# Scatters of rows into expert lists, issued one at a time between the matmuls' accompanying steps

## The chip, the core and the metric

One NeuronCore of a Trainium2 chip runs the kernel. Its engines work side by side, each through its own queue of instructions in order: PE (TensorE, matmuls), DVE (VectorE), ACT (ScalarE), POOL (GpSimd) and SP (SyncE, here only a queue that starts DMA transfers). They wait for one another by semaphores. The metric is the device time of one execution in microseconds (us); less is better.

## The reference

The input is x, 8 batches of 256 tokens with 128 numbers each (2048 tokens in all). Two layers follow one another, each a conditioning step and a feed-forward network (FFN) with 8 experts of 512 hidden units, and each adds its result to x:

```python
x = x + _L0_ffn_ref(_L0_cond_ref(x, ...), ...)   # all 8 experts for every token, weighted by gates above a threshold
x = x + _L1_ffn_ref(_L1_cond_ref(x, ...), ...)   # the 2 best experts of each token

def _L1_ffn_ref(x, gate_w, w1, b1, w2, b2, gamma, beta):
    xn = (x - mu) * jax.lax.rsqrt(var + LN_EPS) * gamma + beta
    probs = jax.nn.softmax(jnp.einsum('bld,de->ble', xn, gate_w), axis=-1)
    w, idx = jax.lax.top_k(probs, TOP_K)                 # TOP_K = 2
    w = w / jnp.sum(w, axis=-1, keepdims=True)
    ...
    h = jax.nn.gelu(jnp.einsum('bld,edh->eblh', xn, w1) + b1[:, None, None, :], approximate=False)
    out_e = jnp.einsum('eblh,ehd->ebld', h, w2) + b2[:, None, None, :]
    return jnp.einsum('ble,ebld->bld', cw, out_e) + residual
```

The first FFN is dense: every expert sees every token. In the second a token needs two experts of eight. The kernel computes only those, and for that it sorts the tokens by expert.

## The kernel before

**Tiling.** The 2048 tokens are 16 tiles of 128. The list UNITS cuts them into five units: units 0, 1 and 2 have four tiles each (512 tokens), units 3 and 4 have two each (256 tokens).

**First FFN (function layer).** For each unit u and each expert e there are four matmuls into the hidden layer (hp, L784), each followed by a GELU on ACT (L786), and four that lead back to 128 numbers (yp, L764, in second). The second half runs one expert behind the first. Accumulate multiplies each yp by the gates of its tokens on DVE (L752) and adds it to acc (L754). The gates come from DRAM as a row copied to all partitions, gbc (L744, a transfer on SP, four buffers). When the last expert of a unit is in, a generator, adapt, is put into the queue behind.

**Steps beside the matmuls.** The function pump is called after each matmul (in the units of two tiles after every second one). It advances the generator at the head of behind by one step. So what adapt does for unit u stands in the program between the matmuls of the unit after it. Adapt(u) transposes acc on PE (fp, L455), applies the adapter of the batch's language (adp, L581, and dp, L588), and normalises twice. Each normalising has a power on POOL: rstd_l and rstd_f, L471. It writes the normalised rows twice into zr, once for each of the two experts (L474, and a copy by ACT), takes a sum on POOL (resid, L609) and writes each row's place in the output into a spare column (copies on POOL, L612). Then it transposes the rows (znp, L617), computes the second layer's logits (L628), picks the two best experts, and counts, with a matmul by a triangle (kp, L659 and L660), the place that each token gets in its expert's list.

**Scatters.** These places, pos, are made on DVE (L674). For each of the two experts and each tile one transfer from POOL, an indirect DMA (L676), writes 128 rows of 520 bytes to xs in DRAM, each to its place. A unit of four tiles has eight scatters, a unit of two has four, 32 in all. They stand in the program one behind the other, four (or two) in one step of adapt and the rest in the next.

**Second FFN.** After unit 2 the lists of 17 full tiles are known, after unit 3 four more, after unit 4 the rest (SLOTS). Each such tile k has one expert. Its rows are loaded from xs (xt, L814) and its expert's weights from DRAM (wt, L822), both on SP, by fetch. The first load of a new stretch of lists (k = 0, 17, 21) waits for all scatters of the units up to it. Fetch(k) also reads the tile's place and expert from the list into registers. Eight tiles are fetched (function early) just ahead of the first FFN's last yp in the program. Then come, for each tile, a transpose (xtp, L829), the hidden layer (hps, L840, with a GELU on ACT, L842), the way back (yps, L849), a sum on DVE (yt, L852), a scaling on ACT (L853), and a scatter of the result to the output's buffer ys from POOL (L854, 36 of them). At the end ys is read back, added up and stored.

**Order.** The program's text gives the order in which work is recorded. A planner then places the instructions on the engines' queues by when it reckons them to be ready, so an instruction that it thinks late can land behind one that was recorded after it, on SP and POOL among others. On the chip each queue is worked off in that fixed order: what waits at its head holds everything behind it.

Of the kernel before, what the change touches and what calls it, by code (L numbers as in the profile page):

```python
# [15 lines left out]
SYNC = mybir.DependencyInfo(mybir.DependencyClass.Sync, mybir.DependencyReason.DATA)  # L16
# [6 lines left out]
P = 128  # L23
# [7 lines left out]
SLOTS = {2: 17, 3: 21, 4: 39}  # L31
E, HC = 8, 4
# [12 lines left out]
SEARCH = 16  # L45
SEARCH_GAP = 3
CHAIN_GAP = 5
GATES_GAP = 16
DRAIN = 4
LEAD = 5  # L50
# [18 lines left out]
def tile_adaln_ffn_d2(ctx: ExitStack, tc: tile.TileContext, x, ptype, lang, cols, b1v,  # L69
                      w10, w20, w11d, w21d, lw1, lw2, lgb, out):  # L70
    nc = tc.nc
# [34 lines left out]
    for e in range(E):  # L106
        t = first.tile([P, HC * P], F32, tag="w1", name=f"w10_{e}")
        nc.sync.dma_start(out=t, in_=w10[e])
        w10s.append(t)
        t = const.tile([P, HC, D], F32, name=f"w20_{e}")  # L110
# [42 lines left out]
    for b in range(B):  # L153
        at = nc.values_load(lgi[0:1, b:b + 1], engines=(SP,), min_val=0, max_val=NL - 1,
                            skip_runtime_bounds_check_because="a language's number")
        for lst, name, src, rows, width in (
# [3 lines left out]
            t = const.tile([rows, width], F32, name=f"{name}_{b}")  # L160
# [19 lines left out]
    fwd, bwd, rows = fwd[:B, :], bwd[:B, :], top[:B, :]  # L180
# [40 lines left out]
    for g in range(NG):  # L221
# [8 lines left out]
        if not g:  # L230
            nc.tensor.matmul(bvp.rearrange("p c a -> p (c a)"), lhsT=ones[:A, :],
                             rhs=diag.rearrange("k c a -> k (c a)"), start=True, stop=True)
# [266 lines left out]
    xs = dram.tile([ROWS + GT * P, RW], F32, name="xs")  # L499
    ys = dram.tile([2 * NT * P, D], F32, name="ys")  # L500
    last, lists, scatters, tiles = [None], {}, [], []
    used = const.tile([P, E], F32, name="used")
    nc.gpsimd.memset(used, 0.0)

# [61 lines left out]
    def adapt(u, acc):  # L566
# [99 lines left out]
        if u in SLOTS:  # L666
            counts = small.tile([P, E], F32, tag="counts", name=f"counts{u}", bufs=2)
            nc.vector.tensor_copy(counts, kp[:, nt, :])
        for s, oh in enumerate((oh1, oh2)):
            wh = small.tile([P, GT, E], F32, tag="s", name=f"wh{u}_{s}")[:, :nt, :]  # L670
            nc.vector.tensor_tensor(wh, oh, at, ALU.mult)
            pos = small.tile([P, GT], I32, tag="pos", name=f"pos{u}_{s}")[:, :nt]
            with nc.allow_low_precision("whole numbers below 2 ** 24"):
                nc.vector.tensor_reduce(pos, wh, AX.X, ALU.add)  # L674
            for t in range(nt):
                move = nc.gpsimd.indirect_dma_start(  # L676
                    out=xs, out_offset=bass.IndirectOffsetOnAxis(ap=pos[:, t:t + 1], axis=0),
                    in_=zr[s][:, t, :], in_offset=None)
                tc.declare_no_dep(move.ins, group="scattered", reason="no two tokens share a row")
                tc.add_to_no_dep_group("scattered", move.ins)  # L680
                scatters.append((u, move.ins.name))
                tc.add_to_no_dep_group(f"scattered {u}", move.ins)
                for v in range(u):
                    if v in SLOTS:
                        tc.declare_no_dep(move.ins, group=f"loads {v}", reason="full tiles get no more rows")
            yield
        if u in SLOTS:

# [10 lines left out]
            if u < NU - 1:  # L699
# [5 lines left out]
                nc.vector.tensor_tensor(new, new, f, ALU.min)  # L705
                nc.vector.tensor_tensor(used, used, new, ALU.add)


    behind = deque()
    waiting = deque()  # L710

    def run(key, steps):
# [6 lines left out]
    def pump():  # L719
        if gd0:  # L720
            n = next(ready)
            if not n:
                gates0.append(gd0[0])
            if waiting and n >= 0 and n % DRAIN == 0:
                waiting.popleft()()
        if behind:
            if next(behind[0], done) is done:
                behind.popleft()

    def finished(key):  # L730
        while key not in done:
            pump()

    def layer(name, act, sources, w1s, w2s, cb1, cb2, gates, before, then, early):

        accs, missing = {}, [E] * NU

        def accumulate(u, e, y, bias):  # L740
            g, o, nt = UNITS[u]
            n, t0 = nt * P, e * NT + g * GT + o
            gbc = work.tile([P, GN], F32, tag="gbc", name=f"gbc_{name}{u}_{e}", bufs=4)[:, :n]
            nc.sync.dma_start(out=gbc, in_=gates[0][t0:t0 + nt, :].rearrange("t p -> (t p)").partition_broadcast(P))  # L744
            begun = u in accs
            if not begun:
                accs[u] = work.tile([P, GN], F32, tag="acc", name=f"acc_{name}{u}", bufs=3)[:, :n]
            part = work.tile([P, GN], F32, tag="part", name=f"part_{name}{u}_{e}")[:, :n] if begun else accs[u]
            if bias is None:
                nc.vector.tensor_tensor(part, y, gbc, ALU.mult)  # L750
            else:
                nc.vector.scalar_tensor_tensor(part, y, bias, gbc, ALU.add, ALU.mult)  # L752
            if begun:
                nc.vector.tensor_tensor(accs[u], accs[u], part, ALU.add)  # L754
            missing[u] -= 1
            if not missing[u]:
                behind.append(run((name, u), then(u, accs[u])))

        def second(u, e, hT):
            nt = UNITS[u][2]  # L760
            n = nt * P
            yp = psy.tile([P, GN], F32, tag="y", name=f"yp_{name}{u}_{e}")[:, :n]
            for c in range(HC):
                nc.tensor.matmul(yp, lhsT=w2s[e][:, c, :], rhs=hT[:, c, :], start=(c == 0), stop=(c == HC - 1))  # L764
                if nt == GT or c % 2:
                    pump()
            b2 = col[:, cb2 + e:cb2 + e + 1]
            if gates:
                accumulate(u, e, yp, b2)
            else:  # L770
                y = scratch(f"y_{name}{u}_{e}").rearrange("p a b -> p (a b)")[:, :n]
                nc.scalar.activation(y, yp, AF.Identity, bias=b2)  # L772
                waiting.append(lambda u=u, e=e, y=y: accumulate(u, e, y, None))


        due = deque()
        for u, (g, o, nt) in enumerate(UNITS):
            n = nt * P
            finished((before, g))
            for e in range(E):  # L780
                hT = work.tile([P, HC, GN], F32, tag="hT", name=f"hT_{name}{u}_{e}")[:, :, :n]
                for c in range(HC):
                    hp = psb.tile([P, GN], F32, tag="big", name=f"hp_{name}{u}_{e}_{c}")[:, :n]
                    nc.tensor.matmul(hp, lhsT=w1s[e][:, c * P:(c + 1) * P], rhs=sources[g][:, o * P:o * P + n],  # L784
                                     start=True, stop=True)
                    nc.scalar.activation(hT[:, c, :], hp, act,  # L786
                                         bias=col[:, cb1 + e * HC + c:cb1 + e * HC + c + 1])
                    if nt == GT or c % 2:
                        pump()
                if due:  # L790
                    second(*due.popleft())
                due.append((u, e, hT))
        early()
        second(*due.popleft())


    def listing(k):

        return min(u for u in SLOTS if k < SLOTS[u])
# [7 lines left out]
    def fetch(k):  # L807
        u = listing(k)
        rows, i = lists[u], k - SLOTS.get(u - 1, 0)
        at = nc.values_load(rows[0:1, 0, i:i + 1], engines=(SP,), min_val=0, max_val=ROWS,  # L810
                            skip_runtime_bounds_check_because="at most ROWS, a difference of counts")
        ek = expert(k, SP)
        xt = work.tile([P, RW], F32, tag="xt", name=f"xt{k}", bufs=LEAD + 2 * AHEAD + 2)
        move = nc.sync.dma_start(out=xt, in_=xs[bass.ds(at, P), :])  # L814
        for v, name in scatters if k in (0, *SLOTS.values()) else ():
            if v <= u:
                tc.add_manual_dep(move.ins, name, SYNC, reason="rows of full tiles")
        for v in range(u + 1, NU):
            tc.declare_no_dep(move.ins, group=f"scattered {v}", reason="full tiles get no more rows")
        tc.add_to_no_dep_group(f"loads {u}", move.ins)  # L820
        wt = first.tile([P, HC * P], F32, tag="w1", name=f"wt{k}")
        nc.sync.dma_start(out=wt, in_=w11d.rearrange("e p w -> (e p) w")[bass.ds(ek * P, P), :])  # L822
        return k, xt, wt
# [12 lines left out]
    def hidden(k, xt, wt, xc, b1):  # L836
        hp = psb.tile([P, HC, P], F32, tag="big", name=f"hps{k}")
        hT = work.tile([P, HC, P], F32, tag="scr", name=f"hs{k}", bufs=NSCR)
        for c in range(HC):
            nc.tensor.matmul(hp[:, c, :], lhsT=wt[:, c * P:(c + 1) * P], rhs=xc, start=True, stop=True)  # L840
        for c in range(HC):
            nc.scalar.activation(hT[:, c, :], hp[:, c, :], AF.Gelu, bias=b1[:, c:c + 1])  # L842
        return k, xt, hT
# [25 lines left out]
    def ahead(k):  # L869

        if k < SURE:
            finished(("first", listing(k)))
            fetched.append(fetch(k))

    def early():
# [91 lines left out]
```

## Time and profile before

| | us |
|---|---|
| runs shown | 388.47, 380.01, 388.97 (median 388.47) |
| the execution that was profiled | 380.68 |
| its span in the profile | 379.0 |
| POOL: 32 scatters into xs (L676) | 31.5 busy, 986 ns each |
| POOL: 36 scatters into ys (L854) | 35.2 busy, 977 ns each |
| PE: hp (L784) and yp (L764) of the first FFN | 121.2 and 120.6 busy |
| PE: hps (L840) and yps (L849) of the second FFN | 39.2 and 39.6 busy |
| PE's last matmul ends | 355.4 |

All times in the profile are from the span's start. A line of the timeline gives start, length, engine, line of the program, operation, what is written and what is read, how often in a row (x4), and in brackets how long the engine was idle before it and what ended that wait. A fp32 matmul shows as two records, or passes. Line numbers are those of the kernel before.

### The profile page before, as it was taken

Reading aid. Unit: us, or ns where it says so; the run is one execution under the profiler, and the core shown is the slowest. Engines: PE = TensorE matmul, PEld = TensorE weight load, DVE = VectorE, ACT = ScalarE, POOL = GpSimd, SP = SyncE. Lnnn points to the kernel's source line nnn. Section 1 sums busy time; section 2 is a strip of 40 time slices with the busy share of each in tenths; the row PEclk is TensorE's granted clock in tenths of the full one; section 3 lists DMA queues with packets and bytes.
Section 4 is the critical chain, followed back from the end, with each engine's and each line's share of the span. In section 5 each row is a group of like instructions: output and inputs, shape, how many; then the busy total and the mean of one; then the engine's idle time right before and its main releaser. Section 6 shows DMA issues by size and latency. Waiting matters only on the chain. (4 is left out here: it accounts for less than half of the span.)

```text
span 379.0 us, 5911 instructions
## 1 busy us (share of the span) xinstructions
PE 345.8 (91%) x1596; PEld 233.0 (61%) x1596; DVE 195.0 (51%) x801; ACT 167.0 (44%) x387; POOL 94.5 (25%) x142
## 2 busy tenths in 40 slices
PE   6799999999999999999999999989989879999900
PEld 6695444444444445445445688857869769999900
DVE  4775565542245675565512474847576644333305
ACT  2166434553542244223443244425635637567800
POOL 8100000000000030650350021262045565444530
PEclk9999999999999999999999999999999998999975
DMA  6935999005222101210130001126543554566136
GB/s 189 382 84 150 368 379 356 4 0 148 69 77 102 56 30 55 63 49 30 56 69 14 28 29 42 36 65 175 151 121 107 162 162 121 168 187 173 47 117 244
DMA packets 33603, 46.12 MB, mean 122 GB/s; under 512 B 5349, under 2 KB 16375, under 8 KB 33569
## 3 DMA queue, kind: packets, MB, share of 16 engines
q1 hardware_dynamic: 29024, 39.26, 34.6%
q0 software_dynamic: 2304, 4.37, 3.2%
q10 hardware_dynamic: 2240, 2.10, 1.6%
q8 instruction: 14, 0.23, 0.3%
q14 instruction: 21, 0.16, 0.1%
HBM read 31.57 MB, written 14.39 MB: 121 GB/s over the span
## 5 line engine op out<-in xcount | busy, mean ns | idle before, releaser
L786 ACT ACTIVATE hT_first<-hp_first,col 128x512 f32<-128x512 f32 (+1 forms) x160 | 93.4, 601 | 103.3 <-PE hp_first L784 102.3
L784 PE MATMUL hp_first<-poolT,w 128*128 128x512 f32 (+1 forms) x320 | 121.2, 513 | 1.3 <-DVE xr L591 0.7
L764 PE MATMUL yp_first<-hT_first,w 128*128 128x512 f32 (+1 forms) x320 | 120.6, 511 | 0.0
L784 PEld LDWEIGHTS hp_first<-poolT,w 128*128 128x128 f32 x320 | 58.8, 190 | 44.2 <-issue 38.2
L764 PEld LDWEIGHTS yp_first<-hT_first,w 128*128 128x128 f32 x320 | 59.0, 190 | 42.5 <-issue 38.6
L676 POOL DMA_INDIRECT xs<-zr,pos x32 | 31.5, 986 | 64.3 <-DVE pos L674 27.9
L842 ACT ACTIVATE hs<-hps,b 128x128 f32<-128x128 f32 x144 | 40.6, 365 | 11.2 <-PE hps L840 5.3
L854 POOL DMA_INDIRECT ys<-yt,xt x36 | 35.2, 977 | 40.9 <-ACT hs L842 28.3
L849 PE MATMUL yps<-w,hs 128*128 x288 | 39.6, 283 | 2.5 <-DVE row L558 2.4
L840 PE MATMUL hps<-xc,wt 128*128 128x128 f32 x288 | 39.2, 280 | 1.1 <-issue 1.1
L849 PEld LDWEIGHTS yps<-w,hs 128*128 128x128 f32 x288 | 35.7, 195 | 4.3 <-issue 3.5
L752 DVE SCALAR_TENSOR_TENSOR part_first<-yp_first,col,gbc_first 128x512 f32<-128x512 f32 (+1 forms) x28 | 17.2, 614 | 40.4 <-PE yp_first L764 39.9
L840 PEld LDWEIGHTS hps<-xc,wt 128*128 128x128 f32 x288 | 36.0, 196 | 0.8 <-issue 0.6
L853 ACT ACTIVATE yt<-yt,xt 128x128 f32<-128x128 f32 x36 | 14.6, 405 | 23.3 <-issue 15.0
L754 DVE TENSOR_TENSOR acc_first<-acc_first,part_first 128x512 f32<-128x512 f32 (+1 forms) x35 | 20.1, 580 | 0.5
L579 POOL MEMSET ha<- 1x512 f32 x5 | 2.6, 516 | 67.6 <-PE dp L588 67.4
L406 POOL DMA_DIRECT2D gd_L<-gT_L x1 | 0.6, 649 | 74.3 <-DVE gT_L L404 74.3
L833 DVE COPY b<-col 128x4 f32 x36 | 7.2, 200 | 23.0 <-ACT hs L842 17.7
L852 DVE TENSOR_TENSOR yt<-yps,b2all 128x128 f32<-128x128 f32 x36 | 10.5, 291 | 14.8 <-PE yps L849 7.1
L831 DVE TENSOR_SCALAR xc<-xtp,col 128x128 f32<-128x128 f32 x36 | 14.4, 401 | 4.0 <-PE xtp L829 2.4
L772 ACT ACTIVATE y_first<-yp_first,col 128x512 f32<-128x512 f32 x8 | 5.5, 687 | 24.2 <-PE yp_first L764 24.2
L420 DVE TENSOR_SCALAR_CACHE_REDUCE fl<-logit,tr 128x128 f32<-128x128 f32 x46 | 13.5, 343 | 0.6
(205 smaller groups left out, 304.2 us busy)
## 6 DMA issues: line engine op xcount, KB each, us to landing
wt<-in_w_dram SPq DMA_DIRECT2D x36, 256.0 KB
xs<-empty SPq DMA_DIRECT2D x1, 8580.0 KB
w<-in_w_dram SPq DMA_DIRECT2D x24, 256.0 KB
gbc_first<-gd_L SPq DMA_DIRECT2D x24, 256.0 KB
xt<-xs SPq DMA_DIRECT2D x36, 65.0 KB
gbc_first<-gd_L SPq DMA_DIRECT2D x16, 128.0 KB
lgb<-in_lgb_dram SPq DMA_DIRECT2D x8, 128.0 KB
yg<-ys ACTq DMA_DIRECT2D x4, 256.0 KB
```

Of the source, the lines that this page charges most:

```text
L676: move = nc.gpsimd.indirect_dma_start(out=xs, out_offset=bass.IndirectOffsetOnAxis(ap=pos[:, t:t + 1], axis=0), in_=zr[s][:, t, :], in_off ...
L752: nc.vector.scalar_tensor_tensor(part, y, bias, gbc, ALU.add, ALU.mult)
L754: nc.vector.tensor_tensor(accs[u], accs[u], part, ALU.add)
L764: nc.tensor.matmul(yp, lhsT=w2s[e][:, c, :], rhs=hT[:, c, :], start=(c == 0), stop=(c == HC - 1))
L784: nc.tensor.matmul(hp, lhsT=w1s[e][:, c * P:(c + 1) * P], rhs=sources[g][:, o * P:o * P + n], start=True, stop=True)
L786: nc.scalar.activation(hT[:, c, :], hp, act, bias=col[:, cb1 + e * HC + c:cb1 + e * HC + c + 1])
L831: nc.vector.tensor_scalar(xc, tp, col[:, C_LG:C_LG + 1], col[:, C_LB:C_LB + 1], ALU.mult, ALU.add)
L840: nc.tensor.matmul(hp[:, c, :], lhsT=wt[:, c * P:(c + 1) * P], rhs=xc, start=True, stop=True)
L842: nc.scalar.activation(hT[:, c, :], hp[:, c, :], AF.Gelu, bias=b1[:, c:c + 1])
L849: nc.tensor.matmul(yp, lhsT=hT[:, c, :], rhs=w21[:, bass.ds(ek, 1), c * D:(c + 1) * D], start=(c == 0), stop=(c == HC - 1))
L853: nc.scalar.activation(yt, yt, AF.Copy, scale=xt[:, D + 1:D + 2])
L854: move = nc.gpsimd.indirect_dma_start(out=ys, out_offset=bass.IndirectOffsetOnAxis(ap=xt.bitcast(I32)[:, D:D + 1], axis=0), in_=yt, in_off ...
```

## The change

The scatters leave the step that computes the places. Adapt puts them into a queue, moves. Every second call of pump (MOVE_GAP) takes one from it and records it, ahead of the step of the generator. The function moved(u) records all that are left of the units up to u: it is called for unit u - 1 before unit u computes its places, and for a tile's unit before that tile is fetched. Each scatter gets one wait more: recent holds the name of the matmul of an expert (hp, yp or the last of a tile's hps) that was recorded last, and the scatter waits until PE has done it. The transfers themselves, their number and their data stay as they are.

```diff
+MOVE_GAP = 2
...
+    moves = deque()
+    recent = [None]
...
+        moved(u - 1)
         for s, oh in enumerate((oh1, oh2)):
...
             for t in range(nt):
-                move = nc.gpsimd.indirect_dma_start(
-                    out=xs, out_offset=bass.IndirectOffsetOnAxis(ap=pos[:, t:t + 1], axis=0),
-                    in_=zr[s][:, t, :], in_offset=None)
-                tc.declare_no_dep(move.ins, group="scattered", reason="no two tokens share a row")
...
+                moves.append((u, pos[:, t:t + 1], zr[s][:, t, :]))
             yield
...
+    def scatter(u, pos, zr):
+        move = nc.gpsimd.indirect_dma_start(
+            out=xs, out_offset=bass.IndirectOffsetOnAxis(ap=pos, axis=0), in_=zr, in_offset=None)
+
+        tc.add_manual_dep(move.ins, recent[0], SYNC, reason="one after another")
+        tc.declare_no_dep(move.ins, group="scattered", reason="no two tokens share a row")
...
+    def moved(u):
+
+        while moves and moves[0][0] <= u:
+            scatter(*moves.popleft())
...
+    beat = itertools.count()
...
     def pump():
...
+        if not next(beat) % MOVE_GAP and moves:
+            scatter(*moves.popleft())
         if behind:
...
-                nc.tensor.matmul(yp, lhsT=w2s[e][:, c, :], rhs=hT[:, c, :], start=(c == 0), stop=(c == HC - 1))
+                mm = nc.tensor.matmul(yp, lhsT=w2s[e][:, c, :], rhs=hT[:, c, :], start=(c == 0), stop=(c == HC - 1))
+                recent[0] = mm.ins.name
...
-                    nc.tensor.matmul(hp, lhsT=w1s[e][:, c * P:(c + 1) * P], rhs=sources[g][:, o * P:o * P + n],
-                                     start=True, stop=True)
+                    mm = nc.tensor.matmul(hp, lhsT=w1s[e][:, c * P:(c + 1) * P], rhs=sources[g][:, o * P:o * P + n],
+                                          start=True, stop=True)
+                    recent[0] = mm.ins.name
...
-            nc.tensor.matmul(hp[:, c, :], lhsT=wt[:, c * P:(c + 1) * P], rhs=xc, start=True, stop=True)
+            mm = nc.tensor.matmul(hp[:, c, :], lhsT=wt[:, c * P:(c + 1) * P], rhs=xc, start=True, stop=True)
+        recent[0] = mm.ins.name
...
         if k < SURE:
             finished(("first", listing(k)))
+            moved(listing(k))
             fetched.append(fetch(k))
```

In the program that this makes, the orders of PE, DVE and ACT are the same as before. On POOL unit 0's scatters stand among unit 1's rstd_l, resid and rstd_f, the last three of unit 2 among unit 3's, and two of unit 4's behind a scatter into ys each. On SP the order of unit 4's gate rows and of the first tiles' loads differs: before, four gate rows stand among the loads of tiles 0 to 5; now three of these stand ahead of the first load, and the fourth (expert 7) behind the weights of tile 7.

More of the change, by code (lines that the diff above doesn't have):

```diff
@@ L675, in adapt @@
             for t in range(nt):
-                move = nc.gpsimd.indirect_dma_start(
-                    out=xs, out_offset=bass.IndirectOffsetOnAxis(ap=pos[:, t:t + 1], axis=0),
-                    in_=zr[s][:, t, :], in_offset=None)
-                tc.declare_no_dep(move.ins, group="scattered", reason="no two tokens share a row")
[L680 to L685, printed above, removed]
+                moves.append((u, pos[:, t:t + 1], zr[s][:, t, :]))
             yield
@@ L706, in adapt @@
                 nc.vector.tensor_tensor(used, used, new, ALU.add)
+    def scatter(u, pos, zr):
[3 more added lines that the diff above has]
+        tc.declare_no_dep(move.ins, group="scattered", reason="no two tokens share a row")
+        tc.add_to_no_dep_group("scattered", move.ins)
+        scatters.append((u, move.ins.name))
+        tc.add_to_no_dep_group(f"scattered {u}", move.ins)
+        for v in range(u):
+            if v in SLOTS:
+                tc.declare_no_dep(move.ins, group=f"loads {v}", reason="full tiles get no more rows")
+    def moved(u):
+        while moves and moves[0][0] <= u:
+            scatter(*moves.popleft())
     behind = deque()
+    beat = itertools.count()
     waiting = deque()
```

## Prediction

> **What bounds the kernel now.** I read the page's busy table first, then the waits of PE, then the timeline of PE, POOL and SP round each wait that is left.
>
> ```profile
> PE 345.8 (91%) x1596; PEld 233.0 (61%) x1596; DVE 195.0 (51%) x801; ACT 167.0 (44%) x387; POOL 94.5 (25%) x142
> PEclk9999999999999999999999999999999998999975
> ```
>
> TensorE is the bound. It works from some 20 us to 356 us, at full clock but for one dent; the last 23 us are the output's way out. So POOL's 31.5 us of scatters (L676, 32 of 986 ns) cost nothing as such. What counts is whether PE waits. From 20 us to 240 us it doesn't (each 20 us stretch of the table by stretches shows 20.00 us busy, or 19.98 and 19.99). Its later waits, between 240 and 340 us, longest first:
>
> ```profile
> PE yps L849 <- DVE row L558: 2.4, 1, 2.4
> PE znp L617 <- DVE zr L474: 1.5, 3, 0.8
> PE xtp L829 <- DVE xc L831: 1.5, 1, 1.5
> PE hps L840 <- issue: 1.1, 1, 1.1
> PE kp L659 <- DVE sofar L653: 0.9, 1, 0.9
> ```
>
> Columns: total us, times, longest. These and a few below 0.8 us are some 9 us. A faster POOL can gain no more; a later transfer can lose as much as it likes. The place to look at is the hand-over from the first FFN to the second. POOL there, then SP:
>
> ```profile
> 252.73 0.96 POOL L676 DMA_INDIRECT xs<-zr,pos  x1 [0.31 <-issue]
> 257.08 0.73 POOL L471 TENSOR_TENSOR rstd_l<-ve_l,nhalf 128x2 f32<-128x2 f32 x1 [3.39 <-DVE ve_l L469]
> 259.92 0.72 POOL L609 TENSOR_TENSOR resid<-x,xr 128x256 f32<-128x256 f32 x1 [2.11 <-DVE xr L598]
> 260.86 0.71 POOL L471 TENSOR_TENSOR rstd_f<-ve_f,nhalf 128x2 f32<-128x2 f32 x1 [0.22 <-DVE ve_f L469]
> ```
>
> ```profile
> 255.28 0.35 SPq L814 DMA_DIRECT2D xt<-xs  x1
> 255.73 0.37 SPq L744 DMA_DIRECT2D gbc_first<-gd_L  x1
> 266.14 0.38 SPq L744 DMA_DIRECT2D gbc_first<-gd_L  x1
> ```
>
> The first is the eighth and last scatter of unit 2. The first tile's load of rows (xt0) waits for it and goes 2.55 us after its start. The last line is the gate row of unit 4, expert 7 (gbc4_7), which DVE and then PE use here:
>
> ```profile
> 277.84 0.47 DVE L752 SCALAR_TENSOR_TENSOR part_first<-yp_first,col,gbc_first 128x256 f32<-128x256 f32 x1
> 278.84 0.44 PE L455 MATMUL fp<-ident,acc_first 128*128 128x128 f32 x2
> ```
>
> Product, sum into acc, then PE's transpose, with nothing between: PE has no slack here, gbc4_7 has 8 us (landing records put it at 269.7 us).
>
> [...] A scatter is 128 x 520 = 66,560 bytes[...] (landing 2.1 to 2.3 us after the start in most of the 31 scatters that have records). [...] rstd_l of unit 1 starts at 164.36 us, behind eight scatters and a memset without a gap. [...] after the waits at 309.6 to 313.4 us the granted clock is 0.86 and 0.80 in the next two 5 us stretches, and eight passes of yps take 1.81 us in place of 1.06.
>
> **The change part by part.** Built, the changed program has the same order on PE, DVE and ACT; the orders of POOL and SP change.
>
> *Units 0 and 1.* Each keeps 8 scatters at 0.96 us plus 0.30 us of issue. Their waits are for matmuls one pair of pumps apart: two 128x512 matmuls, 1.7 us of PE (eight passes, four matmuls, take 3.4 us from start to start). Unit 0's 8 then take some 18 us, to 172, in place of 10. Behind the fifth, which waits for a matmul that PE ends at 163.1 us, stands rstd_l of unit 1; it starts at 164.3 us, as now (164.36), since it gets ahead of the other three. PE has no wait there. Bounds: nothing either way; taken 0. If that cover were gone, a scatter is 1.26 us.
>
> *Unit 2.* The waits are for matmuls that PE ends at about 243.9, 245.6, 247.7, 250.2, 253.6, 256.2, 258.0 and 259.7 us (positions in the new order, read off PE's timeline). But the last three now stand on POOL behind unit 3's rstd_l, resid and rstd_f, and these wait for DVE. So: rstd_l ends 257.8, sixth scatter 258.1 to 259.1; resid ends 260.6, seventh 260.9 to 261.9; rstd_f 261.95 in place of 260.86 (+1.1 us, straight into PE's wait for zr at 262.1); a copy; eighth at 263.2. Landed 2.2 us later and issued 0.4 us after that, as now: **xt0 at 265.8 us in place of 255.28**.
>
> *SP.* The planner answers to the late xt0: three gate rows go ahead of it, and gbc4_7 now stands behind xt0 to wt7, sixteen issues. SP's own pace in the stretch above is 0.91 us from an xt to its wt and 0.83 us back: 8 x 0.91 + 7 x 0.83 + 0.44 = 13.5 us. gbc4_7 is issued at 279.3 us. Its like landed 2.7 to 3.7 us after issue between 240 and 270 us; 3.4 us [...]: 282.7 us. The tiles' loads themselves are late without harm: xt3 is issued at 271 us and used at 278.7, wt7 at 278.9 and used near 292.
>
> *PE.* DVE's product starts at 282.8 in place of 277.84 and the transpose at 283.8 in place of 278.84: **+5.0 us**, in which the 1.1 us above is contained (PE comes to this point at 279.9 and stands for 3.9 us). [...] 1.5 us more of waiting for xc follows. So half clock [...] taken +1.3, bounds 0 and 1.7. Everything of unit 4 hangs on acc and shifts with it, so nothing of this is given back there. The +5.0 itself has bounds 2 and 7 (landing, and some 0.1 us an issue on sixteen issues).
>
> *Unit 3.* Waits for matmuls that end by 277 us at the latest, POOL idle: 0.
>
> *Unit 4.* Four scatters, now with two outputs' scatters (ys) between them, each waiting for a tile's hps that PE has done. Two ys leave 2.5 us earlier; the last scatter ends near 313 in place of 310.4. xt21, which waits for it, goes at 317.88 now: 2 to 3 us of slack, 0. The page has a stand of DVE, ACT and PE at 308 to 313 us just beside this burst (3.5 us on PE, 1.7 us by clock). It names a DVE row that PE doesn't need, and I can't see its cause. Bounds: -5.2 if the burst makes it, 0 if not; taken 0.
>
> Sum: 380.68 us (span 379.0 and 1.7 about it) + 5.0 + 1.3 = **387.0 us**. The median of the runs shown, 388.47, is of another kind of execution than the profiled one: 380.01 stands beside 388.47 and 388.97. I sum from the profiled one.
>
> **Rivals.** (1) *Given back*: the slip happens, but without the burst the stand at 308 us goes: 387.0 - 5.2 = 381.8. For it: the stand starts between the third and fourth scatter. Against: bursts of eight at 153, 185 and 243 us made none. It decides if nothing above 2 us is left between 308 and 320 us of the old count. (2) *Faster*: the extra 8.5 us of two of the three runs come from such stands at bursts, and spacing ends them, while gbc4_7 lands by 278 us because SP runs faster than reckoned: 376 to 380. Against: it must make up 4 us in sixteen issues. It decides if PE shows no wait above 2 us after 240 us. (3) *Slower still*: the waits on PE hold POOL where I took them as past. An unpaid 2 us at rstd_f or at a ys goes through DVE to PE[...]: 391 to 396. It decides if POOL waits for PE at an L676 with other work queued behind. (4) *It does nothing*: the matmuls waited for are done when POOL arrives, as at most of unit 2's and 4's. The order on SP has changed all the same, so this too gives 387.
>
> **How the numbers follow.** A measurement of this kernel can tell about 2% from no change: 388.3 us from the profiled execution. The slip as summed, (4) included: 0.52, at 385 to 390, half on each side of that. (3): 0.16, slower. (1): 0.12, within. (2): 0.20, faster. So slower 0.26 + 0.16 = 0.42, within 2% 0.26 + 0.12 = 0.38, faster 0.20. The time is the likeliest case's, 387; the likeliest case alone is 385 to 390; the range 379 to 396 takes in (1), the top of (2) and (3).
>
> **What would show it.** xt0 issued near 266 us; gbc4_7 after the eighth wt, near 279; one DVE wait for gbc_first of some 5 us; a new PE wait of 3 to 4 us at fp (L455 of the old count), with a clock under 1 after it. Wrong if xt0 goes before 258, or gbc4_7 has landed by 278; the sum is then 380 or below. If fp waits as said and the total is still 382, it is rival 1.

## The result, and the profile after

| | kernel before | changed kernel |
|---|---|---|
| median, us (lowest to highest) | 385.21 (380.01 to 389.14) | 385.85 (383.82 to 387.39) |
| profiled execution, us (its span) | 380.68 (379.0) | 385.96 (384.3) |
| ratio, with its 95% interval | | **1.0124 [1.009, 1.0158]** |

The change makes the kernel about 1.2% slower, which is less than the 2% that I had put as the bound. The ratio, here and below, leaves out disturbed executions (here three of the six of the kernel before, from 388.47 us up, and none of the changed kernel), so a median can stand far from its ratio. The time forecast was 387.0 us.

The page of the changed kernel, busy time and clock:

```profile
PE 349.5 (91%) x1596; PEld 236.7 (62%) x1596; DVE 195.6 (51%) x801; ACT 167.1 (43%) x387; POOL 97.0 (25%) x142
...
PEclk9999999999999999999999999999989999899975
```

TensorE does the same 1596 matmuls and is still the bound. Its busy time is 3.7 us longer without a matmul more, so some of them ran slower: the clock came up later at the start, and it has two dents now instead of one. From the list of TensorE's waits (total us, times, longest):

```profile
PE fp L456 <- DVE acc_first L770: 4.8, 1, 4.8
...
PE hps L858 <- issue: 2.2, 3, 1.2
PE znp L620 <- DVE zr L475: 2.0, 3, 1.0
...
PE kp L662 <- DVE sofar L656: 0.9, 1, 0.9
```

The first line is new. The wait of 2.4 us at yps and that of 1.5 us at xtp, which stood in the list of before, are gone. The timeline of POOL where unit 2's scatters end (start, duration; in brackets the idle time before it and what ended it):

```profile
255.79 0.96 POOL L704 DMA_INDIRECT xs<-zr,pos  x1 [2.19 <-issue]
256.78 0.74 POOL L472 TENSOR_TENSOR rstd_l<-ve_l,nhalf 128x2 f32<-128x2 f32 x1
257.70 1.03 POOL L704 DMA_INDIRECT xs<-zr,pos  x1 [0.18 <-PE hp_first L801]
...
261.61 0.72 POOL L472 TENSOR_TENSOR rstd_f<-ve_f,nhalf 128x2 f32<-128x2 f32 x1
...
262.65 1.30 POOL L704 DMA_INDIRECT xs<-zr,pos  x1 [0.17 <-issue]
```

The scatters stand among unit 3's small operations, and the eighth starts at 262.65 us, where it started at 252.73. SP's timeline, the first tile's rows and then the end of the first sixteen tile loads:

```profile
265.54 0.35 SPq L832 DMA_DIRECT2D xt<-xs  x1
...
279.55 0.01 SPq L840 DMA_DIRECT2D wt<-in_w_dram  x1
280.29 0.01 SPq L760 DMA_DIRECT2D gbc_first<-gd_L  x1
```

The last line is the gate row of unit 4 and expert 7, issued at 280.29 us instead of 266.14. DVE and PE there:

```profile
283.55 0.48 DVE L768 SCALAR_TENSOR_TENSOR part_first<-yp_first,col,gbc_first 128x256 f32<-128x256 f32 x1 [4.89 <-DMA gbc_first<-gd_L]
284.57 0.44 PE L456 MATMUL fp<-ident,acc_first 128*128 128x128 f32 x2 [4.81 <-DVE acc_first L770]
...
286.30 1.91 PE L858 MATMUL hps<-xc,wt 128*128 128x128 f32 x8
```

DVE waits for the gate row alone, PE for DVE, and behind this stand (a stretch in which an engine does nothing) eight passes of hps take 1.91 us in place of 1.06: half clock.

Since both kernels issue the same matmuls in the same order, the two traces can be laid beside each other matmul by matmul. The changed kernel's start is later by:

| at (time in the trace of before) | later by, us | what lies in between |
|---|---|---|
| 12 us, and all the way to 239 us | 2.05 | the first 12 us: the clock came up at 12.0 us instead of 6.4 |
| 267 to 278 us | 0.77 | two stands of before at 252 and 255 us (0.61 and 0.69 us) are not there; znp waits 0.5 us more |
| 287 to 303 us | 5.7 | +4.97: the stand at fp and the half clock, less the wait of xtp |
| 317 to 320 us | 1.5 | before has its own stand and half clock at 309 to 317 us |
| 329 us | 5.75 | the changed kernel has stands and a half clock of its own at 315 to 329 us |
| last matmul | 5.43 | it ends at 359.96 us before (not at 355.4, as the table and the prediction have it), at 365.40 now |

So of 5.43 us, 2.05 have nothing to do with the change. **Its own price in this pair of profiles is 3.4 us.** The lowest executions of the two kernels, 380.01 and 383.82 us, lie 3.8 us apart, which is 1.0%; some of the measured 1.2% is then likely to be the start as well.

### The profile page after: what moved, and what is told of

Its sections match the earlier page's. It is cut to its first block, busy times and chain, and to the rows that moved or that the text cites. A ratio compares the mean times of both kernels' runs of the same rounds, so it can differ in the third digit from the quotient of the medians.

```text
span 384.3 us, 5923 instructions
## 1 busy us (share of the span) xinstructions
PE 349.5 (91%) x1596; PEld 236.7 (62%) x1596; DVE 195.6 (51%) x801; ACT 167.1 (43%) x387; POOL 97.0 (25%) x142
## 5 line engine op out<-in xcount | busy, mean ns | idle before, releaser
L704 POOL DMA_INDIRECT xs<-zr,pos x32 | 33.8, 1055 | 71.6 <-PE yp_first L780 30.7
L858 PE MATMUL hps<-xc,wt 128*128 128x128 f32 x288 | 40.7, 284 | 2.2 <-issue 2.2
L858 PEld LDWEIGHTS hps<-xc,wt 128*128 128x128 f32 x288 | 37.0, 200 | 2.4 <-issue 2.1
L872 ACT ACTIVATE yt<-yt,xt 128x128 f32<-128x128 f32 x36 | 14.6, 405 | 22.7 <-issue 13.5
L421 DVE TENSOR_SCALAR_CACHE_REDUCE fl<-logit,tr 128x128 f32<-128x128 f32 x46 | 13.5, 343 | 0.6
```

The costliest lines, as they stand in the source:

```text
L704: move = nc.gpsimd.indirect_dma_start(out=xs, out_offset=bass.IndirectOffsetOnAxis(ap=pos, axis=0), in_=zr, in_offset=None)
L858: mm = nc.tensor.matmul(hp[:, c, :], lhsT=wt[:, c * P:(c + 1) * P], rhs=xc, start=True, stop=True)
L872: nc.scalar.activation(yt, yt, AF.Copy, scale=xt[:, D + 1:D + 2])
```

## Experiments

Theory 1 says: the wait added to unit 2's last scatters makes xt0 late; SP is in order and has the gate row behind the tiles' loads; PE waits for the gate row. Rivals: the lost time comes from POOL's waits as such, from unit 4's spaced scatters, or from chance at the start. Four kernels on one chip first; the kernel before took 380.1 us there (median of eleven).

### e1: the one gate row ahead of the tiles' loads

```diff
+        def gate_row(u, e):
...
+            nc.sync.dma_start(out=gbc, in_=gates[0][t0:t0 + nt, :].rearrange("t p -> (t p)").partition_broadcast(P))
+            return gbc
...
-            gbc = work.tile([P, GN], F32, tag="gbc", name=f"gbc_{name}{u}_{e}", bufs=4)[:, :n]
...
+            gbc = ahead_of.pop((u, e)) if (u, e) in ahead_of else gate_row(u, e)
...
+        ahead_of[due[0][:2]] = gate_row(*due[0][:2])
         early()
```

> The changed kernel, but the gate row of unit 4, expert 7 is recorded ahead of the first eight tiles' loads, so that SP issues it after the first weight and not after the eighth. Theory 1 (the loss is that one late gate row): xt0 still goes at about 265.5 us, the gate row at about 267 and lands by 271; DVE's wait for gbc_first (4.9 us) and PE's wait at fp (4.8 us) go to 0, the clock stays full there; time 379 to 381 us, ratio to before 0.993 to 1.003. Rival (the waits on PE hold POOL, or the late tile loads themselves cost): the PE wait moves to another place of some 4 us and the ratio stays at 1.008 to 1.016.

Measured: 379.74 us (378.14 to 385.04), **0.9974 [0.9945, 1.0004]**. SP's timeline of this kernel, and nothing at fp in its list of waits:

```profile
270.52 0.35 SPq L839 DMA_DIRECT2D xt<-xs  x1
...
271.88 0.37 SPq L760 DMA_DIRECT2D gbc_first<-gd_L  x1
```

In this profile the start is late (6.7 us behind that of before from 25 us on, see the last section), so 270.52 is 263.8 by the clock of before. The tiles' rows are as late as in the changed kernel, all 32 scatters wait for matmuls as in the changed kernel, and the loss is gone. The late tile loads do no harm here; the one gate row does.

### e2, e3, e4: which unit's spacing it is

```diff
                 moves.append((u, pos[:, t:t + 1], zr[s][:, t, :]))
+            if u == 2:
+                moved(u)
```

This is e2: unit 2's scatters at once, the others spaced. In e3 the condition is `u != 2` (only unit 2 spaced), in e4 `u != 4` (only unit 4 spaced).

> The changed kernel, but unit 2's eight scatters are recorded in the step that makes their places; units 0, 1, 3 and 4 stay spaced and keep their waits on PE. SP's order is then that of before. Theory 1: xt0 near 255 to 258 us, no wait at fp, ratio 0.985 to 1.003 (below 1 if spacing unit 4 shortens the stand at 308 us). Rival (the waits on PE in the other units cost the time): ratio 1.008 to 1.016.

> The reverse: only unit 2's scatters are spaced and wait for PE, the four other units' are recorded at once as before. Theory 1: the whole loss is here, gate row issued at about 280 us, PE wait of 4 to 5 us at fp, ratio 1.010 to 1.020. Rival: ratio 0.997 to 1.004. If spacing unit 4 gives something back in the changed kernel, this one is up to 1 % slower than it.

> Only unit 4's four scatters are spaced and wait for a tile's hps, with two scatters of outputs between them. Theory A (the burst of four makes the stand of DVE, ACT and PE near 308 us): no PE wait above 1 us between 300 and 325 us and full clock, 375 to 377 us, ratio 0.985 to 0.992. Theory B (the stand has another cause): the stand of 3 to 4 us with a dent of the clock is there or at a place nearby, ratio 0.997 to 1.003.

| | median, us | ratio | xt0 | gate row | wait at fp |
|---|---|---|---|---|---|
| e2 | 379.66 | 0.9955 [0.9919, 0.9991] | 255.86 | 266.73 | none |
| e3 | 389.49 | 1.0078 [1.0038, 1.0118] | 263.62 | 278.16 | 4.8 us |
| e4 | 382.3 | 1.0042 [0.9997, 1.0088] | 260.98 (start 5.2 us late) | 271.85 | none |

The gate row of e3 on SP's timeline:

```profile
278.16 0.07 SPq L762 DMA_DIRECT2D gbc_first<-gd_L  x1
```

and the top of e3's list of waits:

```profile
PE fp L456 <- DVE acc_first L772: 4.8, 1, 4.8
```

Unit 2's spacing alone brings the loss, and with the other units' spacing alone (e2) the kernel is slightly faster than the kernel before. e3's ratio is less than the 1.010 to 1.020 that I expected, and it rests on two executions (382.71 and 383.52 us); its profile starts as that of before does, so the two can be laid beside each other as they are, and e3's last matmul is 3.1 us later. e4's interval takes in no change. The stand of before at 308 to 313 us was thought to go with unit 4's spacing. It does not: e4 has seven smaller ones (0.24 to 0.82 us) between 315 and 329 us instead. From the start of unit 4's kp product to the end of the last matmul the six profiles so far take 55.9 to 57.5 us, spaced or not. What makes these stands was open, and e9 to e14 come back to it.

Leaving the added wait out and keeping the rest needed no run: the program that results is that of before to the instruction. Where the steps stand in the kernel's text changes nothing here; only the wait does.

### e5 to e8: the start filled, and the dose

e1 to e4 showed that profiles differ by up to 6.7 us before anything of the change has run. These four, on a second chip, fill TensorE's first microseconds:

```diff
+    warm = const.tile([P, P], F32, name="warm")
+    nc.vector.memset(warm, 0.0)
     make_identity(nc, ident)
...
-    pass_time(5, ident, ident)
+    pass_time(8, warm, warm)
...
         if not g:
+            pass_time(1, warm, warm)
             nc.tensor.matmul(bvp.rearrange("p c a -> p (c a)"), lhsT=ones[:A, :],
```

e7 adds e1's edit, with the gate row recorded ahead of the seventh tile's load: behind six tiles, not eight and not none. e8 adds e2's.

> The kernel before with its first six microseconds of TensorE filled: a tile of zeros is written by VectorE as its first instruction, and nine idle matmuls on it (instead of five on the identity) start at about 1.3 us rather than 2.6, so that no pause of TensorE is left ahead of the small bvp product. All else keeps its order. Theory S (executions of one kernel differ by when the clock is first granted in full, 5.9 to 25.5 us in the six profiles so far, and by nothing else): the clock comes full by about 5 us in this profile, the stretch up to 20 us costs at most what it did in the profile of before, the median is 379 to 380.5 us and its six executions lie within 1.5 us. Rival (the clock's start follows something else than TensorE's pauses, or the spread has another source): the executions spread over 4 us and more as before, and the median is unchanged or higher.

> The changed kernel with the same filled start. Theory 1 (the late gate row costs about 3.4 us net of the start): 383 to 384 us, 1.007 to 1.011 of the kernel before with the filled start, with a stand of 4.8 us before the fp transpose and a stretch at half clock behind it. Rival (the median of 1.012 was the start's chance): within 1 us of the kernel before with the filled start, though the stand is there, because other stands give it back.

> As the last, with the one gate row of unit 4 and expert 7 recorded behind six tiles' loads on SP's queue instead of eight. Theory 1: two pairs of tile and weight issues at 1.72 us each come off the gate row's wait: issued at 276.9 instead of 280.3, VectorE's product 3.4 us earlier, the stand before the fp transpose 4.8 - 3.4 = 1.4 us[...]. The time 4 to 5 us below the changed kernel with the filled start. Rival (the stand is set by something else on VectorE or by the eighth scatter alone): stand and time stay as they were with eight tiles ahead.

> Unit 2's scatters at once, the other units' spaced behind matmuls, with the filled start: the version meant to beat both. If its gain in the first job (0.9955) was real and its worst executions (385 to 386 us) were the start's, the median is 376 to 377 us, all executions within 1.5 us, and the ratio to the kernel before about 0.99. Rival (its gain was a good start in some executions): equal to the kernel before with the filled start within 1 us.

| | median, us (range) | ratio to the kernel before |
|---|---|---|
| e5 before, start filled | 382.53 (379.7 to 389.59) | 1.0014 [0.9981, 1.0048] |
| e6 changed, start filled | 384.36 (383.93 to 392.43) | 1.0079 [1.0046, 1.0112] |
| e7 gate row behind six | 378.84 (377.74 to 385.84) | **0.995 [0.9912, 0.9988]** |
| e8 unit 2 at once | 382.54 (378.21 to 388.79) | **0.9959 [0.9939, 0.998]** |

Theory S is half right at best. In the four profiles the clock is full at 4.8 to 7.2 us and the first 40 us agree within 0.3 us, so the fill does what it was made for. But the executions of e5 lie as far apart as those of before, and the median gains nothing. The spread has a source that the fill doesn't reach (the last section has what is on record of it).

e8 repeats e2's ratio, but not the 376 to 377 us that I expected of it, nor executions within 1.5 us of one another.

The dose came out as expected. The timeline of DVE and PE in e6, gate row issued at 277.79 us:

```profile
282.23 0.48 DVE L771 SCALAR_TENSOR_TENSOR part_first<-yp_first,col,gbc_first 128x256 f32<-128x256 f32 x1 [5.66 <-DMA gbc_first<-gd_L]
...
283.25 0.69 PE L459 MATMUL fp<-ident,acc_first 128*128 128x128 f32 x2 [5.57 <-DVE acc_first L773]
```

and in e7, issued at 274.25:

```profile
278.09 0.48 DVE L777 SCALAR_TENSOR_TENSOR part_first<-yp_first,col,gbc_first 128x256 f32<-128x256 f32 x1 [1.23 <-DMA gbc_first<-gd_L]
...
279.11 0.44 PE L459 MATMUL fp<-ident,acc_first 128*128 128x128 f32 x2 [1.14 <-DVE part_first L777]
```

Issued 3.5 us earlier, used 4.1 us earlier, and the stand is 1.14 us (1.4 expected). Behind e6's stand the clock is half for 6.8 us; in e7 no half stretch follows before the last matmul. The median is 5.5 us below e6's (4.9 us by the two ratios; 4 to 5 expected). The rival, that DVE or the eighth scatter sets the stand, is out. Laid matmul by matmul with the start taken off, e7 ends 6.0 us before e6, and e1 6.0 us before the changed kernel. So the gate row costs more than the 3.4 us of the whole change: with the row moved up, the last matmul comes 2.7 us earlier in e1 than in the kernel before, and 2.8 us earlier in e7 than in e5, though all scatters are spaced. By their ratios, 0.9974 and 0.995, the gain is 0.3 to 0.5%, and e1's interval takes in no change.

### e9 to e14: what the stands beside unit 4's scatters are

e9 is e5, and e10 is e7, with unit 4's four scatters left out, so unit 4's tokens get nothing from the experts' tiles; the result buffer is set to zero early so that rows never written are defined.

```diff
+    nc.sync.dma_start(out=ys.rearrange("(p m) d -> p m d", p=P), in_=empty[:, 0:1, :D].to_broadcast([P, 2 * NT, D]))
...
-            for t in range(nt):
+            for t in range(nt) if u != 4 else ():
```

> The kernel before with the filled start, without the four scatters of unit 4's rows (they are left out, so unit 4's tokens get nothing from the experts' tiles; the rows of the result buffer are set to zero early, by one more transfer of 2 MB among the first weights). All other orders are as they were. Theory B (the four scatters in a row, 5.1 us of POOL in a stage that has one output's scatter every 2 us, make the stand of DVE and PE at 308 to 313 us): no gap of TensorE above 1 us between 305 and 330 us, the stage from unit 4's kp to the last matmul shorter by 3 to 5 us than in the two profiles with the burst. Rival (the stand has nothing to do with the scatters): gaps of 2.5 to 4 us in sum near the same matmuls, and the stage as long as it was, 56 us.

> The changed kernel with the filled start and the gate row behind six tiles, without unit 4's four scatters (left out in the same way, and the result buffer set to zero in the same way). Theory B: the scattered small stands at 312 to 316 us go (1.06, 0.48, 0.25 and 0.23 us in the profile with them), the stage from unit 4's kp on is as long as in the last run within 1 us, and the time is 375 to 377 us. Rival: stands of 2 us in sum remain between 305 and 330 us.

Measured: e9 367.8 us, 0.9986 [0.995, 1.0022]; e10 369.83 us, 1.0034 [1.0014, 1.0054]. Neither profile has a stand of PE between 305 and 330 us, as Theory B has it, and both take 49.8 us from unit 4's kp product to the last matmul's end. But this job ran on a third chip, on which the kernel before took 369.18 us. Against that, leaving the scatters out is worth nothing. The two observations don't fit together unless the chips differ, and no profile of before is at hand from that one. e10 stands 2.94 us at fp where e7, with the same order, stood 1.14: SP took 1.23 us over the gate row's issue instead of 0.38, and DVE, which waited for the row, had it at 279.65 us instead of 278.09.

So both kernels once more with profiles, and the omission with its control, all on one chip (a fourth). e13 is e5 with the buffer set to zero; e14 is e9 again.

> The kernel before itself, once more, with its own profile. Ratio 1 within 0.4%: this shows what the comparison resolves. If this job's times of before are near 369 us, its profile shows no gap of TensorE above 1 us between 305 and 330 us and no wait of xtp for xc at 280 us (then those belong to the chip, not to the program); if they are near 380 us, it shows 2 to 5 us of them.

> The changed kernel itself, once more. Theory 1: the gate row is issued behind eight tiles' loads at 279 to 281 us whatever the chip, fp waits 4.5 to 6 us, half clock follows in most executions. The ratio is 1.008 to 1.013 where before takes 380 us; where before takes 369 us and has no stands of its own for the slip to take the place of, it is larger, 1.015 to 1.02. Rival: the ratio falls to 1 within 0.4% on a chip without the stands.

> The kernel before with the filled start and the result buffer set to zero early, with unit 4's four scatters in a row. The control for the next run. Theory B: gaps of TensorE of 2.5 to 4 us in sum between 305 and 330 us, whichever chip. Rival (the chip): none where before takes 369 us.

> The same without unit 4's four scatters (they are left out, so unit 4's tokens get nothing from the experts' tiles). Theory B: 3 to 5 us less than the control and no gap above 1 us. Rival (the chip): within 1 us of the control and with the same gaps, where there are any.

| | median, us | ratio to the kernel before (381.94) |
|---|---|---|
| e11 the kernel before | 381.96 | 0.9986 [0.9953, 1.0019] |
| e12 the changed kernel | 388.1 | 1.011 [1.0077, 1.0143] |
| e13 control | 381.8 | 0.9997 [0.9972, 1.0023] |
| e14 without unit 4's scatters | 374.75 | **0.9811 [0.9754, 0.9868]** |

e11, the kernel before against itself, comes out at 0.9986, and its interval takes in 1. e12 repeats the loss, with a stand of 5.61 us at fp and a half clock of 6.8 us behind it. e13 and e14 settle the question for this chip. The timeline of PE in e13:

```profile
310.62 0.27 PE L844 MATMUL hps<-xc,wt 128*128 128x128 f32 x1 [0.65 <-issue]
312.07 0.27 PE L844 MATMUL hps<-xc,wt 128*128 128x128 f32 x1 [1.17 <-issue]
...
314.06 2.05 PE L853 MATMUL yps<-w,hs 128*128 x8 [1.72 <-DVE row L562]
```

Single passes, with two pauses that no semaphore explains, and then a wait for DVE, which itself had done nothing for 5.01 us, while POOL scatters from 306.1 to 310.9 us. The table by stretches (length, busy time of PE, PEld, DVE, ACT and POOL, then the granted clock), e13:

```profile
300.00:330.00 30.00, 25.44 (x200) 24.74 (x200) 13.70 (x69) 15.81 (x54) 15.11 (x17) 0.89 0.57 157
```

and e14:

```profile
300.00:330.00 30.00, 29.06 (x256) 28.57 (x256) 15.60 (x75) 20.00 (x71) 13.59 (x14) 1.00 0.63 177
```

Without the four scatters 256 passes go through in these 30 us instead of 200. The one pause left is kp's own, 0.93 us. Theory B holds here: the scatters make the stand, and with the half clock it starts they cost 7 us, more than the 3 to 5 expected (e14's ratio rests on three executions, 374.42 to 374.92 us). Leaving out is not spacing, though: with the same four spaced by tiles (e4, e6, e7, e12) the kernel still has stands there, in smaller pieces. That these too are the scatters' doing is likely, but no run on this chip leaves them out of a spaced kernel.

## Why the prediction was right or wrong

**The mechanism was right.** xt0 was predicted for 265.8 us and came at 265.54; the gate row behind the eighth weight, 279.3 and 280.29; a DVE wait of some 5 us for gbc_first, 4.89; a new wait at fp of 3 to 4 us with a clock under 1 after it, 4.81 us with eight passes at 1.91 us. e1, e3 and e7 show that this is the whole of the loss. That these times were met within 1 us is in part luck: the changed kernel's include the late start of 2.05 us, as point 1 says. Units 0 and 1 cost nothing, as said: between 12 and 239 us the distance of the two traces doesn't change by more than 0.03 us. There POOL did slip, though not where I looked: with the start taken off, unit 1's rstd_l is at 165.2 us instead of 164.36 and its rstd_f at 171.65 instead of 170.00, and PE has no wait behind them.

**The likeliest class was wrong: slower by over 2% (0.42) against a measured 1.2%.** Two terms of the sum were too large, and the weighing added to it.

1. *PE's +5.0.* With the late start (2.05 us) taken off, fp is at 282.5 us, which is +3.7. The step that failed is the one on unit 2: rstd_f was to slip by 1.1 us, since the sixth and seventh scatters stand in front of it. With the start taken off it ran at 259.56 us, 1.3 us *earlier* than in the kernel before. The cause is not on POOL. DVE's first sum of unit 3 in the trace of before:

```profile
255.24 0.42 DVE L591 TENSOR_TENSOR xr<-dp,x 128x256 f32<-128x256 f32 x1 [2.84 <-PE hp_first L784]
```

and in the changed kernel:

```profile
253.05 0.42 DVE L594 TENSOR_TENSOR xr<-dp,x 128x256 f32<-128x256 f32 x1 [0.20 <-PE dp L591]
```

   Before had a stand of 2.84 us on DVE here, and two on PE, beside and behind the last of unit 2's eight scatters:

```profile
252.17 0.70 PE L784 MATMUL hp_first<-poolT,w 128*128 128x256 f32 x2 [0.61 <-issue]
...
255.72 1.56 PE L784 MATMUL hp_first<-poolT,w 128*128 128x256 f32 x6 [0.69 <-DVE xr L591]
```

   The changed kernel has none of them. This is hardly chance: of the profiles but the two of the third chip, all eight with unit 2's scatters in a row show such stands of PE between 250 and 262 us (0.5 to 1.4 us in sum), and none of the six with unit 2 spaced does. The price of spacing is 0.5 us more at znp, which waits for zr. I had counted these waits within the 9 us that can be gained, and then priced the edit that moves the work beside them as if they stayed. Everything from rstd_l on came earlier than reckoned for it, xt0 too: its 265.54 us is 263.5 with the start taken off. That the forecast was met to 0.3 us is the late start's doing. A second error goes the other way: from xt0 to the gate row SP took 14.75 us, and not the 13.5 of its earlier pace. Without it fp would have been near +2.5.

2. *The clock's +1.3, and the xc wait.* That half clock would follow the stand was an estimate. It did, for 3.41 us from 285.03 us, and cost its full 1.7 us. But "1.5 us more of waiting for xc follows" was wrong: while PE stood at fp, DVE made xc, and the 1.49 us wait of before is gone. A stand swallows the waits that come next on the same engine if what they wait for goes on. Together the two came to 0.0 instead of +1.3.

So at 287 us +3.7 us was measured where +6.3 was predicted.

3. *Unit 4, taken as 0.* In the sum this was right: from 303 us to the end the distance changes by 0.2 us. The reasoning was not. I let bursts of eight at 153, 185 and 243 us, which I took to have made no stand, speak against the burst at 305. The one at 243 us has the stands of point 1, in the trace that I had, and e14 shows that the one at 305 us makes its own. And the lower bound, -5.2 "if the burst makes it", took spacing for removal. Rival 1 falls with that: before's stand of 3.5 us and its half stretch give way to 2.7 us in five pieces and another half stretch at 326 us.

4. *The base.* 380.68 us was a fair base: it is near the lowest of the executions, and the kernel before took 380.1 us on the chip of e1 to e4. That the other two of the three runs lay 8 us higher I had, in rival 2, put down to bursts. No such execution of the kernel before was profiled, so that isn't settled. But the long executions of the spaced kernels that were, e1 and e12, lost 6.7 and 7.0 us before 26 us, where nothing is scattered yet. Rival 2 is out as worded, for PE waits 4.81 us at fp, although e2, e7 and e8 do end slightly faster than before.

5. *The weighing.* 387.0 over 380.68 is 1.0166, inside the 2%. I split the slip case in halves at 388.3 us and then laid rival 3 (0.16, slower) on top. Nothing of rival 3 came, whose 391 to 396 us was an estimate: POOL does wait for PE with rstd_l or resid queued behind it, and e1, with all these waits, loses nothing. With the two terms right, 380.68 + 3.7 = 384.4 us, 1.0098; that is near the measured ratio, and the likeliest class would have been no change that 2% can tell.

**The price of the change alone**, in three pairs of profiles laid matmul by matmul with the start taken off: 3.4 us here, 3.2 us (e6 against e5) and 3.6 us (e12 against e11).

## What to carry to other kernels

When a transfer is made later, look at what an in-order queue has behind it, not at the transfer: eight tiles' loads came 5 to 8 us late (start taken off) and cost nothing, and the one 128 KB row behind them cost some 6 us, of which the spacing gave some 2.7 back; two tiles fewer ahead of it took the stand from 5.57 to 1.14 us. When a new stand is priced, strike out the waits of the same engine that it will cover, and those beside the work that is moved away, before adding it up. Compare profiles matmul by matmul and take the start's difference off first, or chance at the start passes for the change.

## What the runs showed of the hardware

**The clock's start.** TensorE runs at half speed first, and the moment from which the trace's clock record has full speed differs from execution to execution of programs whose start is the same: 5.9, 6.3, 6.4, 11.1, 12.0, 22.7, 25.5 and 25.7 us in eight profiles. The late ones lose up to 7.0 us, nearly 2% of the time, by then. The kernel before, PE's timeline:

```profile
8.15 0.98 PE L203 MATMUL xa<-col,xT 128*128 128x40 f32 x8
...
15.86 2.32 PE L190 MATMUL idle<-xT,sl 128*128 128x256 f32 x10
```

and e12:

```profile
10.01 1.77 PE L204 MATMUL xa<-col,xT 128*128 128x40 f32 x8
...
21.27 4.47 PE L191 MATMUL idle<-xT,sl 128*128 128x256 f32 x10
```

The same ten passes take 4.47 us instead of 2.32, more than 20 us into the kernel. In e4 the clock was full from 5.7 to 9.1 us and then half again until 22.7. In e12 the trace shows no pause of TensorE over 0.05 us from 6.81 to 20.46 us, and the clock stayed half until 25.7 us. Why it did is not known.

The fill of TensorE from 1.1 us on gave a full clock at 4.1 to 7.2 us in eight profiles of eight, yet left the spread of the times as it was. The granted clock, which is on record for each execution, tells in part where the time goes instead. It leaves out what lies before the first full clock: e1's profile, full from 25.5 us, has 0.978. Of the 24 executions of the kernel before on the second chip that took over 385 us, 22 have 0.969 to 0.978, as the short ones have; they can be late starts. The 23 of e5, e8 and e13 over 385 us have 0.948 to 0.963. So with the fill the long executions have more half clock after the first full clock. e4's profile has 0.963, with its half stretch of 13.7 us near the start; where it lies in the long executions with the fill stays open, since none was profiled.

**The clock in the middle.** Before the last matmul's end the clock's record has half clock from 313.63 to 317.04 us in the kernel before, and from 285.03 to 288.44 and 325.99 to 329.40 us in the changed kernel: 3.41 us each, begun 307.20, 273.07 and 314.03 us after the first full clock, some 90, 80 and 92 times that length. In the 3.41 us just ahead of them TensorE stood for 2.88, 2.98 and 1.73 us; in e5 (half from 253.98 us) it was 1.38 us, in e12 (half from 288.55 us) all 3.41. Yet 1.85 us in the 3.41 us from 278.2 us on left the clock of the changed kernel full. What decides between the two isn't shown. (All this is by the trace's records, in which the ends of matmuls are modelled.)

**Scatters on POOL beside instructions of the other engines.** Around unit 4's scatters PE, DVE and SP all pause where the profile shows nothing that they wait for. PE's single passes come 1.43 to 1.45 us apart (e5, e11 and e13), and in the trace of before four of SP's small instructions between two transfers take 0.69 to 0.70 us each between 306 and 312 us, where the median of their kinds is 0.03 and 0.05 us. Taking the scatters out takes the pauses out. Unit 2's burst makes a smaller pause of the same look (point 1 above). The bursts of eight at 153 and 185 us make none (in before TensorE is busy for all 60.00 us from 140 to 200 us); SP issues no loads of tiles yet then. What holds the engines was not found, and no run separates the scatters from the loads beside them. One rival was not tried. The page of the profile lists DMA queue q8 as "instruction", and in before, e5, e11 and e13 a transfer of 16 KB on it starts 1.1 to 1.7 us ahead of PE's first pause beside unit 4's scatters (before: 307.9 and 309.6 us), so the engines may be short of instructions. But such transfers also pass without a pause (changed kernel, 252.1 us; e14, 304.9 us).

**Chips.** In the experiments the kernel before took 380 to 383 us (medians) on three chips and 369 us on another, where leaving out unit 4's scatters gained nothing. It had no profile there. The profile of e9 from that chip, with unit 2's scatters in a row, has no pause of PE between 250 and 262 us, so the chip may be free of these pauses; no run there has unit 4's scatters and a profile.
